# Token lists of the experts from 32-column one-hot matrices in four column groups, and a last expert in two halves

## The chip, the cores and the metric

The kernel runs on one core of one Trainium2 chip. The metric is device time in microseconds (us) of one execution, given as the median of several runs. The engines are named as in the profile: PE is TensorE's matmul, PEld its weight load, DVE VectorE, ACT ScalarE, POOL GpSimd, SP the engine whose queue carries most DMAs.

## What is computed

The reference is one adaptive-layer-norm block of a transformer: attention over 8 sequences of 1024 tokens with 256 features, then a mixture of 8 experts. The change lies in the mixture:

```python
logits = xf @ router_w + router_b                 # 8192 tokens x 8 experts
scores = softmax(logits)
G, idx = top_k(scores.T, 512)                     # each expert chooses 512 tokens
toks = xf[idx]
h1 = relu(einsum('ekh,ehf->ekf', toks, w1) + b1)  # 256 -> 1024
eo = einsum('ekf,efh->ekh', h1, w2) + b2          # 1024 -> 256
y = zeros.at[idx].add(eo * G)
```

An expert needs the list of its 512 tokens; the order within a list is free, since results are added back by token.

## The kernel before, in words

Up to about 3270 us the kernel does attention, the second layer norm and the router; up to 3333 us it searches, for all experts at once, the score that 512 tokens reach (fifteen rounds on DVE and PE), and numbers the tokens chosen. Each chosen token of an expert then has a slot from 0 to 511; a token that isn't chosen has slot -1. Tokens stand on 128 partitions, in 64 columns per expert: 4 blocks `i` (`KT`) by 16 columns `c` (`C`).

From there on the expert stage turns slots into a list. A slot is split into a low part `lo` (L954, 7 bits) and a high part `hi` (L955, 2 bits).

- `entries(e)` makes, on DVE, `at_hi` (L970, a one-hot of the high part over 4 values) and `ids` (L975 and L978): the number of the token, as the first token of its column (`first`) and its partition (`part`), put at the place of its high part. There are 8 columns for each of the 64.
- `choose(e, i)` makes `hot` (L985), a one-hot of the low part over 128 values for 16 columns, and multiplies: 16 matmuls (L992) with `hot` as the weights (128 columns) and `ids` as the moving operand (8 columns) add into `pi`, 128 slots x 8. It is called four times for an expert.
- `gather(e)` copies `pi` to `parts` (L1001), adds its halves to the token numbers `tok` (L1003), and issues four indirect DMAs on POOL (L1007), each fetching 128 rows with the normalized features, the router's scores and the gate.
- `turn(e)` transposes the rows on PE (L1020) and copies them to `xT` (L1023, DVE).
- `inner(e, f)`, 8 steps for an expert: two float32 matmuls (L1031) of 512 moving columns, each of them two passes in the profile, then bias and relu on ACT (L1035) into `h1`.
- `outer(e, j)`, for each of four groups of 128 tokens: 8 float32 matmuls (L1041) of 256 columns, then on DVE the bias (L1046) and the weighting by score and gate (L1047) into `eo`, and on POOL an indirect DMA (L1050) that adds `eo` to the output in DRAM. These scatters write the same tensor, and each waits for the landing of the one before.

The order of instructions in this stage is written by hand (`tc.manual_schedule()`): each engine issues in the order in which the code calls it. Ahead of the loop come `entries`, four `choose`, `gather` and `turn` of expert 0. In the period of expert `e`, the four `choose(e + 1, ...)` follow the inner steps 1, 3, 4 and 6 (counted from 0), `gather(e + 1)` follows the inner product, and `turn(e + 1)` follows the third outer step. Expert weights come in by DMA four experts ahead. In PSUM, `pi` has one bank, `px` two, `ph` three and `po` two. The setup of the constants (`iota_lo`, `iota_hi`, `part`, `first`, made on POOL) stands outside the written order, and a planner places it.

Of the kernel before, what the change touches and what calls it, by code (L numbers as in the profile page):

```python
# [28 lines left out]
F32 = mybir.dt.float32  # L29
BF16 = mybir.dt.bfloat16  # L30
I32 = mybir.dt.int32
AF = mybir.ActivationFunctionType
ALU = mybir.AluOpType
AX = mybir.AxisListType
# [3 lines left out]
P = 128  # L38
# [4 lines left out]
def adaln_block(  # L43
# [15 lines left out]
    nc = tc.nc  # L59
    B, S, D = x.shape  # L60
    H, _, _, N = w_qkv.shape
    E, _, F = w1.shape
    K = 512
# [5 lines left out]
    FC = F // P  # L69
    KT = K // P  # L70
# [7 lines left out]
    ident = const.tile([P, P], F32, name="ident")  # L78
# [14 lines left out]
    b1_sb = const.tile([P, E, FC], F32, name="b1_sb")  # L93
# [557 lines left out]
    def free_slot(g, behind=False):  # L651
        while g in taken or g % 4 == 0 or behind != (g % 4 == 3):
            g += 1
        taken.add(g)
        return g
# [9 lines left out]
    for b in range(B):  # L665
# [16 lines left out]
        if b + 1 < B:  # L682
# [3 lines left out]
            for t in range(NT):  # L686
                g = free_slot(64 * (b + 1) + 19 + 4 * t, True)
# [3 lines left out]
                if t % 2:  # L691
                    g = free_slot(g + 2, True)
                    at(g, "m2", out_turn, ps_m, b, t - 1)
                    g = free_slot(g + 1)
# [15 lines left out]
    with tc.manual_schedule():  # L710
# [20 lines left out]
        g = -1  # L731
# [96 lines left out]
    ex_w = {}  # L828

    def load_expert(e):  # L830
        w1_sb = wts.tile([P, KC, F], F32, tag="w1", name=f"w1_{e}")
        nc.sync.dma_start(w1_sb, w1[e].rearrange("(k p) f -> p k f", p=P))
        w2_sb = wts.tile([P, FC, D], F32, tag="w2", name=f"w2_{e}")
        nc.scalar.dma_start(w2_sb, w2[e].rearrange("(f p) d -> p f d", p=P))
        ex_w[e] = w1_sb, w2_sb
# [4 lines left out]
    rt = ctx.enter_context(tc.tile_pool(name="route", bufs=1))  # L840
    C = NTT // KT
    lo = rt.tile([P, KT, E, C], I32, name="lo")
    hi = rt.tile([P, KT, E, C], I32, name="hi")
    iota_lo = rt.tile([P, P], F32, name="iota_lo")
    iota_hi = rt.tile([P, KT], F32, name="iota_hi")
    part = rt.tile([P, 1], F32, name="part")
    first = rt.tile([P, KT, C], F32, name="first")
    b2_sb = rt.tile([P, E, D], F32, name="b2_sb")
# [5 lines left out]
    with tc.tile_pool(name="search", bufs=2) as se, tc.tile_pool(  # L854
        name="pos", bufs=1
    ) as po_, tc.tile_pool(name="se_ps", bufs=2, space=PSUM) as sps, tc.tile_pool(
        name="pos_ps", bufs=1, space=PSUM
    ) as pps:
        for dst, pattern, mult in (
            (iota_lo, [[1, P]], 0), (iota_hi, [[1, KT]], 0), (part, [[0, 1]], 1),  # L860
            (first, [[P, KT], [P * KT, C]], 0),
        ):
            i = po_.tile(list(dst.shape), I32, name=f"i_{dst.name}")
            nc.gpsimd.iota(i, pattern=pattern, base=0, channel_multiplier=mult)
            nc.gpsimd.tensor_copy(dst, i)

        whole = po_.tile([P, E, C], F32, name="whole")
        nc.gpsimd.memset(whole, 1.0)
# [24 lines left out]
        for s in range(15):  # L893
            bit = 28 - 2 * s
            cnt = se.tile([P, 3], F32, tag="cnt", name=f"cnt{s}")
            for k in range(3):
# [3 lines left out]
                    op0=ALU.is_ge, op1=ALU.add, accum_out=cnt[:, k : k + 1],  # L900
# [47 lines left out]
        for i in range(KT):  # L948
            nc.tensor.transpose(p_no[:, i, :], up[:, i * P : (i + 1) * P], ident)
        slot = po_.tile([P, KT, E, C], I32, name="slot")  # L950
        nc.vector.tensor_scalar_add(
            slot, p_no.rearrange("p i (e c) -> p i e c", e=E), -1.0
        )
        nc.vector.tensor_single_scalar(lo, slot, P - 1, op=ALU.bitwise_and)  # L954
        nc.vector.tensor_single_scalar(  # L955
            hi, slot, P.bit_length() - 1, op=ALU.arith_shift_right
        )

    ew = ctx.enter_context(tc.tile_pool(name="ework", bufs=2))
    ps_ids = ctx.enter_context(tc.tile_pool(name="ps_ids", bufs=1, space=PSUM))  # L960
    ps_x = ctx.enter_context(tc.tile_pool(name="ps_x", bufs=2, space=PSUM))
    ps_h = ctx.enter_context(tc.tile_pool(name="ps_h", bufs=3, space=PSUM))
    ps_o = ctx.enter_context(tc.tile_pool(name="ps_o", bufs=2, space=PSUM))
    out_rows = out.rearrange("b s d -> (b s) d")
    chosen = {}

    def entries(e):

        at_hi = ew.tile([P, KT, C, KT], F32, tag="at_hi", name=f"at_hi{e}")
        nc.vector.tensor_tensor(  # L970
            at_hi, hi[:, :, e, :].unsqueeze(3).to_broadcast([P, KT, C, KT]),
            iota_hi.unsqueeze(1).unsqueeze(1).to_broadcast([P, KT, C, KT]), ALU.is_equal,
        )
        ids = ew.tile([P, KT, C, 2 * KT], BF16, tag="ids", name=f"ids{e}")
        nc.vector.tensor_tensor(  # L975
            ids[:, :, :, :KT], at_hi, first.unsqueeze(3).to_broadcast([P, KT, C, KT]), ALU.mult
        )
        nc.vector.tensor_scalar(ids[:, :, :, KT:], at_hi, part, None, op0=ALU.mult)  # L978
        chosen[e] = ids, ps_ids.tile([P, 2 * KT], F32, tag="pi", name=f"pi{e}")

    def choose(e, i):

        ids, pi = chosen[e]
        hot = ew.tile([P, C, P], BF16, tag="hot", name=f"hot{e}_{i}")
        nc.vector.tensor_tensor(  # L985
            hot,
            iota_lo.unsqueeze(1).to_broadcast([P, C, P]),
            lo[:, i, e, :].unsqueeze(2).to_broadcast([P, C, P]),
            ALU.is_equal,
        )  # L990
        for c_ in range(C):
            nc.tensor.matmul(  # L992
                pi, hot[:, c_, :], ids[:, i, c_, :],
                start=(i == 0 and c_ == 0), stop=(i == KT - 1 and c_ == C - 1),
            )

    def gather(e):

        pi = chosen[e][1]
        parts = ew.tile([P, 2 * KT], F32, tag="parts", name=f"parts{e}")  # L1000
        nc.vector.tensor_copy(parts, pi)  # L1001
        tok = ew.tile([P, KT], I32, tag="tok", name=f"tok{e}")
        nc.vector.tensor_add(tok, parts[:, :KT], parts[:, KT:])  # L1003
        rows = []
        for j in range(KT):
            row = ew.tile([P, WIDE], F32, tag=f"row{j}", name=f"erow{e}_{j}")
            nc.gpsimd.indirect_dma_start(  # L1007
                out=row, out_offset=None, in_=rows_d,
                in_offset=bass.IndirectOffsetOnAxis(ap=tok[:, j : j + 1], axis=0),
            )  # L1010
            rows.append(row)
        chosen[e] = tok, rows

    def turn(e):
        tok, rows = chosen[e]
        xT = ew.tile([P, KC, K], F32, tag="xT", name=f"xT{e}")
        for k in range(KC):
            px = ps_x.tile([P, K], F32, tag="px", name=f"px{e}_{k}")
            for j in range(KT):
                nc.tensor.transpose(  # L1020
                    px[:, j * P : (j + 1) * P], rows[j][:, k * P : (k + 1) * P], ident
                )
            nc.vector.tensor_copy(xT[:, k, :], px)  # L1023
        h1 = ew.tile([P, FC, K], F32, tag="h1", name=f"h1_{e}")
        chosen[e] = tok, rows, xT, h1

    def inner(e, f):
        tok, rows, xT, h1 = chosen[e]
        ph = ps_h.tile([P, K], F32, tag="ph", name=f"ph{e}_{f}")
        for k in range(KC):  # L1030
            nc.tensor.matmul(  # L1031
                ph, ex_w[e][0][:, k, f * P : (f + 1) * P], xT[:, k, :],
                start=(k == 0), stop=(k == KC - 1),
            )
        nc.scalar.activation(h1[:, f, :], ph, AF.Relu, bias=b1_sb[:, e, f : f + 1])  # L1035

    def outer(e, j):
        tok, rows, xT, h1 = chosen[e]
        po = ps_o.tile([P, D], F32, tag="po", name=f"peo{e}_{j}")
        for f in range(FC):  # L1040
            nc.tensor.matmul(  # L1041
                po, h1[:, f, j * P : (j + 1) * P], ex_w[e][1][:, f, :],
                start=(f == 0), stop=(f == FC - 1),
            )
        eo = ew.tile([P, D], F32, tag="eo", name=f"eo{e}_{j}", bufs=4)
        nc.vector.tensor_add(eo, po, b2_sb[:, e, :])  # L1046
        nc.vector.scalar_tensor_tensor(  # L1047
            eo, eo, rows[j][:, D + e : D + e + 1], rows[j][:, ROW:], op0=ALU.mult, op1=ALU.mult
        )
        nc.gpsimd.indirect_dma_start(  # L1050
            out=out_rows,
            out_offset=bass.IndirectOffsetOnAxis(ap=tok[:, j : j + 1], axis=0),
            in_=eo, in_offset=None, compute_op=ALU.add,
        )


    with tc.manual_schedule():
        entries(0)
        for i in range(KT):
            choose(0, i)  # L1060
        gather(0)
        turn(0)
        for e in range(E):
            more = e + 1 < E
            if more:
                entries(e + 1)
            for f in range(FC):
                inner(e, f)
                if more and f in (1, 3, 4, 6):
                    choose(e + 1, (1, 3, 4, 6).index(f))  # L1070
            if more:
                gather(e + 1)
            for j in range(KT):
                outer(e, j)
                if more and j == 2:
                    turn(e + 1)
            if e + 4 < E:
                load_expert(e + 4)


# [29 lines left out]
```

## Time and profile before

| | us |
|---|---|
| median of 3 runs | 3617.36 (3617.17 to 3618.96) |
| profiled execution | 3616.66 |
| its span, first to last instruction | 3614.9 |
| PE busy | 3458.4 (96%) |
| DVE busy | 2898.9 (80%) |
| POOL busy | 2660.0 (74%) |
| ACT busy | 2439.8 (67%) |
| first instruction of the expert stage starts | 3333.62 |
| inner product of the first and of the last expert starts | 3354.68, 3575.0 |
| last scatter is issued | 3607.31 |

All positions are microseconds from the start of the span. In a line of instructions, the name `hot<-iota_lo,lo` says which tile is written from which; the shapes are partitions x elements per partition; "x16" is how many instructions the line holds. Brackets give the idle time of the engine ahead of the line, and what ended it. A busy matmul includes the pipeline's latency, so the pace of PE is read from starts, not from durations. The granted TensorE clock is 1.0 at full rate; in the search and at the start of the expert stage it is 0.5.

### The profile page before, as it was taken

The numbers are of one execution on the slowest core, as the hardware profiler recorded it, in microseconds if no ns is written. First come the engines' busy times: TensorE is split into PE (matmuls) and PEld (weight loads), VectorE is DVE, ScalarE is ACT, GpSimd is POOL, SyncE is SP. The second block draws the span as 40 slices with busy tenths as digits, with TensorE's granted clock in tenths as the row PEclk, the third lists the DMA queues.
The fourth block names the chain that finished last, engine by engine and source line by source line (L and its number), as shares of the span: only waits on it lengthen the run. The fifth ranks groups of instructions, "written<-read, shape, count | busy, mean of one in ns | idle before, by whom it ended". The sixth has DMA issues, their size and how long they took to land. (4 is left out here: it accounts for less than half of the span.)

```text
span 3614.9 us, 54207 instructions
## 1 busy us (share of the span) xinstructions
PE 3458.4 (96%) x20622; PEld 1456.3 (40%) x20622; DVE 2898.9 (80%) x3641; ACT 2439.8 (67%) x2988; POOL 2660.0 (74%) x1537
## 2 busy tenths in 40 slices
PE   7999999999999999999999999999999999982898
PEld 3333333343433443344433434334334344342565
DVE  5888888888888888888888888888888888857442
ACT  4777777777777777777777777777777777730111
POOL 2778777887788887977888788877888877851332
PEclk9999999999999999999999999999999999995999
DMA  3010012011111113111211112011201112133332
GB/s 77 13 42 31 25 32 67 29 45 45 59 50 35 51 49 64 31 39 51 61 46 44 41 44 62 30 52 48 67 29 45 45 59 49 51 87 121 94 100 41
DMA packets 189652, 185.39 MB, mean 51 GB/s; under 512 B 48952, under 2 KB 167240, under 8 KB 189264
## 3 DMA queue, kind: packets, MB, share of 16 engines
q1 hardware_dynamic: 173616, 160.29, 15.5%
q0 software_dynamic: 7168, 12.72, 1.7%
q10 hardware_dynamic: 8608, 8.92, 0.8%
q8 instruction: 162, 2.65, 0.3%
q14 instruction: 98, 0.80, 0.1%
HBM read 127.06 MB, written 63.21 MB: 53 GB/s over the span
## 5 line engine op out<-in xcount | busy, mean ns | idle before, releaser
L457 POOL TENSOR_TENSOR acc<-acc,p 128x1024 f32<-128x1024 f32 x762 | 1806.6, 2371 | 361.2 <-ACT p L429 328.1
L376 ACT COPY p<-s 128x1024 f32<-128x1024 f32 x1024 | 997.2, 1020 | 417.8 <-PE s L367 407.7
L426 DVE TENSOR_TENSOR p<-p,less 128x1024 f32<-128x1024 f32 x1024 | 1206.8, 1210 | 32.5 <-PE less L423 30.0
L381 DVE TENSOR_TENSOR top<-top,s 128x1024 f32<-128x1024 f32 x768 | 936.9, 1220 | 276.5 <-ACT p L376 236.2
L429 ACT ACTIVATE p<-p 128x1024 f32<-128x1024 f32 x1024 | 1042.8, 1058 | 73.7 <-DVE p L426 73.4
L367 PE MATMUL s<-qk,qk 64*128 64x512 f32 x4096 | 1025.1, 612 | 34.0 <-DVE parts L404 31.0
L438 PE MATMUL av<-p,v 128*64 128x512 f32 x4096 | 967.1, 593 | 1.8 <-ACT oT L447 1.8
L367 PEld LDWEIGHTS s<-qk,qk 64*128 64x128 f32 x4096 | 358.7, 186 | 527.8 <-issue 241.2
L332 PE MATMUL pq<-hT,wq 128*64 128x512 f32 x2048 | 498.4, 608 | 2.7 <-ACT v L354 2.1
L438 PEld LDWEIGHTS av<-p,v 128*64 128x64 f32 x4096 | 280.5, 137 | 461.4 <-issue 366.2
L454 POOL TENSOR_TENSOR acc<-p,p 128x1024 f32<-128x1024 f32 x127 | 301.8, 2376 | 178.0 <-ACT p L429 178.0
L332 PEld LDWEIGHTS pq<-hT,wq 128*64 128x64 f32 x2048 | 124.8, 136 | 342.4 <-issue 210.8
L349 PE MATMUL pv<-wq,hT 128*64 128x256 f32 x2048 | 249.3, 385 | 0.7 <-ACT qk L337 0.7
L1035 ACT ACTIVATE h<-ph,b_sb 128x512 f32<-128x512 f32 x64 | 44.1, 689 | 274.7 <-PE ph L1031 274.7
L396 DVE TENSOR_REDUCE tt<-tt 128x8 f32<-128x1024 f32 x128 | 157.4, 1230 | 69.6 <-PE tt L388 69.5
L548 PE MATMUL po<-wo,ot 128*64 128x256 f32 x1792 | 205.7, 382 | 0.0
L349 PEld LDWEIGHTS pv<-wq,hT 128*64 128x64 f32 x2048 | 135.6, 136 | 153.3 <-issue 65.9
L381 DVE TENSOR_TENSOR top<-p,s 128x1024 f32<-128x1024 f32 x128 | 155.8, 1217 | 14.5 <-ACT p L376 14.5
L388 PEld LDWEIGHTS tt<-ident,top 128*128 128x128 f32 x1024 | 109.6, 140 | 106.6 <-DVE top L381 105.8
L519 POOL TENSOR_TENSOR oT<-oT,rb 128x1024 f32<-128x1024 f32 x63 | 150.1, 2382 | 3.0 <-DMA rb<-rden_d 3.0
L548 PEld LDWEIGHTS po<-wo,ot 128*64 128x64 f32 x1792 | 123.6, 137 | 66.1 <-issue 9.4
L388 PE MATMUL tt<-ident,top 128*128 128x128 f32 x1024 | 139.9, 280 | 2.6 <-DVE top L381 2.6
(166 smaller groups left out, 2357.3 us busy)
## 6 DMA issues: line engine op xcount, KB each, us to landing
rb<-rden_d SPq DMA_DIRECT2D x128, 256.0 KB
oT_d<-oT SPq DMA_DIRECT2D x62, 512.0 KB
ot<-oT_d SPq DMA_DIRECT2D x56, 512.0 KB
rows_d<-row SPq DMA_DIRECT2D x64, 132.0 KB
rows_d<-gb_d SPq DMA_DIRECT2D x8, 1024.0 KB
w<-in_L_ffn_w_dram ACTq DMA_DIRECT2D x8, 1024.0 KB
w<-in_L_ffn_w_dram SPq DMA_DIRECT2D x8, 1024.0 KB
lnx<-in_L_attn_inputs_dram SPq DMA_DIRECT2D x28, 256.0 KB
```

Of the source, the lines that this page charges most:

```text
L332: nc.tensor.matmul(pq[m * N : (m + 1) * N, :], wq_of(k, a, 2 * p + m), hTs[b][:, k, sl], start=(k == 0), stop=(k == KC - 1),)
L349: nc.tensor.matmul(pv[m * N : (m + 1) * N, i, :], hTs[b][:, k, t0 : t0 + N], wq_of(k, 2, 4 * g, 4), start=(k == 0), stop=(k == KC - 1),)
L367: nc.tensor.matmul(ps[:, j, :], kt[r, c * P : (c + 1) * P], qt[r, h * QB : (h + 1) * QB], start=True, stop=True,)
L376: nc.scalar.copy(probs[u, c], ps)
L381: nc.vector.tensor_tensor(tops[u], probs[u, 0] if c == 1 else tops[u], ps, ALU.max)
L388: nc.tensor.transpose(turned[u][:, 4 * j + t, :], top[:, j, t * P : (t + 1) * P], ident)
L426: nc.vector.tensor_tensor(probs[u, c], probs[u, c], less[u], ALU.add)
L429: nc.scalar.activation(probs[u, c], probs[u, c], AF.Exp)
L438: nc.tensor.matmul(avs[u][j * N : (j + 1) * N, :], v[:, c, hh * N : (hh + 1) * N], pT[:, j, :], start=(c == 0), stop=(c == NT - 1),)
L454: nc.gpsimd.tensor_tensor(sums[u], pts[0], pts[1], ALU.add)
L457: nc.gpsimd.tensor_tensor(sums[u], sums[u], pt, ALU.add)
L548: nc.tensor.matmul(po[m * N : (m + 1) * N, :], ot[:, p, m * N : (m + 1) * N], wo[:, p, :], start=(p == 0), stop=(p == NP - 1),)
```

## The change

The slot is split at 5 bits rather than 7. `hot` becomes one tile for the whole expert, a one-hot of the low part over 32 values, and `at_hi` and `ids` grow to 16 values of the high part: `ids` has 32 columns for each of the 64. `choose(e)` is called once. Its 64 matmuls have 32 weight columns each and are dealt out to four column groups of PE (`tile_position`), each of which adds up a quarter of the columns in 32 partitions of `pi`. The result is copied as bfloat16 to `parts` (exact, since its numbers are small or multiples of 128 with few bits). `gather(e)` first folds: 8 matmuls with the 0/1 matrix `fold` (32 columns, made once from the identity) add the four groups and both halves of the number, and put 4 high values into each group of 32 partitions, so that `tok` again is 128 x 4. `tok` is then one copy from PSUM.

In the loop, `choose(e + 1)` follows inner step 4 and `gather(e + 1)` inner step 5. The last expert leaves the loop: it does all inner steps for its first 256 tokens, then their two outer steps, then the same for the other 256.

```diff
@@ setup
-    iota_lo = rt.tile([P, P], F32, name="iota_lo")
-    iota_hi = rt.tile([P, KT], F32, name="iota_hi")
+    LO = 32
+    HI = K // LO
+    iota_lo = rt.tile([P, LO], F32, name="iota_lo")
+    iota_hi = rt.tile([P, HI], F32, name="iota_hi")
+    fold = rt.tile([P, LO], BF16, name="fold")
...
-            (iota_lo, [[1, P]], 0), (iota_hi, [[1, KT]], 0), (part, [[0, 1]], 1),
+            (iota_lo, [[1, LO]], 0), (iota_hi, [[1, HI]], 0), (part, [[0, 1]], 1),
...
+        nc.vector.tensor_reduce(
+            fold, ident.rearrange("p (g l) -> p l g", l=LO), AX.X, ALU.max
+        )
...
-        nc.vector.tensor_single_scalar(lo, slot, P - 1, op=ALU.bitwise_and)
+        nc.vector.tensor_single_scalar(lo, slot, LO - 1, op=ALU.bitwise_and)
         nc.vector.tensor_single_scalar(
-            hi, slot, P.bit_length() - 1, op=ALU.arith_shift_right
+            hi, slot, LO.bit_length() - 1, op=ALU.arith_shift_right
         )
@@ def entries(e)
-        at_hi = ew.tile([P, KT, C, KT], F32, tag="at_hi", name=f"at_hi{e}")
+        hot = ew.tile([P, KT, C, LO], BF16, tag="hot", name=f"hot{e}")
         nc.vector.tensor_tensor(
-            at_hi, hi[:, :, e, :].unsqueeze(3).to_broadcast([P, KT, C, KT]),
-            iota_hi.unsqueeze(1).unsqueeze(1).to_broadcast([P, KT, C, KT]), ALU.is_equal,
-        )
-        ids = ew.tile([P, KT, C, 2 * KT], BF16, tag="ids", name=f"ids{e}")
+            hot, iota_lo.unsqueeze(1).unsqueeze(1).to_broadcast([P, KT, C, LO]),
+            lo[:, :, e, :].unsqueeze(3).to_broadcast([P, KT, C, LO]), ALU.is_equal,
+        )
+        at_hi = ew.tile([P, KT, C, HI], BF16, tag="at_hi", name=f"at_hi{e}")
         nc.vector.tensor_tensor(
-            ids[:, :, :, :KT], at_hi, first.unsqueeze(3).to_broadcast([P, KT, C, KT]), ALU.mult
-        )
-        nc.vector.tensor_scalar(ids[:, :, :, KT:], at_hi, part, None, op0=ALU.mult)
-        chosen[e] = ids, ps_ids.tile([P, 2 * KT], F32, tag="pi", name=f"pi{e}")
-
-    def choose(e, i):
-        ids, pi = chosen[e]
-        hot = ew.tile([P, C, P], BF16, tag="hot", name=f"hot{e}_{i}")
+            at_hi, hi[:, :, e, :].unsqueeze(3).to_broadcast([P, KT, C, HI]),
+            iota_hi.unsqueeze(1).unsqueeze(1).to_broadcast([P, KT, C, HI]), ALU.is_equal,
+        )
+        ids = ew.tile([P, KT, C, 2 * HI], BF16, tag="ids", name=f"ids{e}")
         nc.vector.tensor_tensor(
-            hot,
-            iota_lo.unsqueeze(1).to_broadcast([P, C, P]),
-            lo[:, i, e, :].unsqueeze(2).to_broadcast([P, C, P]),
-            ALU.is_equal,
-        )
-        for c_ in range(C):
-            nc.tensor.matmul(
-                pi, hot[:, c_, :], ids[:, i, c_, :],
-                start=(i == 0 and c_ == 0), stop=(i == KT - 1 and c_ == C - 1),
-            )
+            ids[:, :, :, :HI], at_hi, first.unsqueeze(3).to_broadcast([P, KT, C, HI]), ALU.mult
+        )
+        nc.vector.tensor_scalar(ids[:, :, :, HI:], at_hi, part, None, op0=ALU.mult)
+        chosen[e] = hot, ids
+
+    def choose(e):
+        hot, ids = chosen[e]
+        pi = ps_ids.tile([P, 2 * HI + KT], F32, tag="pi", name=f"pi{e}")
+        for i in range(KT):
+            for c_ in range(C):
+                r = c_ % 4 * LO
+                nc.tensor.matmul(
+                    pi[r : r + LO, : 2 * HI], hot[:, i, c_, :], ids[:, i, c_, :],
+                    start=(i == 0 and c_ < 4), stop=(i == KT - 1 and c_ >= C - 4),
+                    tile_position=(0, r),
+                )
+        parts = ew.tile([P, 2 * HI], BF16, tag="parts", name=f"parts{e}")
+        nc.vector.tensor_copy(parts, pi[:, : 2 * HI])
+        chosen[e] = parts, pi
 
     def gather(e):
-        pi = chosen[e][1]
-        parts = ew.tile([P, 2 * KT], F32, tag="parts", name=f"parts{e}")
-        nc.vector.tensor_copy(parts, pi)
+        parts, pi = chosen[e]
+        for g in range(4):
+            r = g * LO
+            for i in range(2):
+                nc.tensor.matmul(
+                    pi[r : r + LO, 2 * HI :], fold, parts[:, i * HI + g * KT : i * HI + (g + 1) * KT],
+                    start=(i == 0), stop=(i == 1), tile_position=(0, r),
+                )
         tok = ew.tile([P, KT], I32, tag="tok", name=f"tok{e}")
-        nc.vector.tensor_add(tok, parts[:, :KT], parts[:, KT:])
+        nc.vector.tensor_copy(tok, pi[:, 2 * HI :])
@@ def inner
-    def inner(e, f):
+    def inner(e, f, t0=0, n=K):
...
-                ph, ex_w[e][0][:, k, f * P : (f + 1) * P], xT[:, k, :],
+                ph, ex_w[e][0][:, k, f * P : (f + 1) * P], xT[:, k, t0 : t0 + n],
...
-        nc.scalar.activation(h1[:, f, :], ph, AF.Relu, bias=b1_sb[:, e, f : f + 1])
+        nc.scalar.activation(
+            h1[:, f, t0 : t0 + n], ph, AF.Relu, bias=b1_sb[:, e, f : f + 1]
+        )
@@ the written order
         entries(0)
-        for i in range(KT):
-            choose(0, i)
+        choose(0)
         gather(0)
         turn(0)
-        for e in range(E):
-            more = e + 1 < E
-            if more:
-                entries(e + 1)
+        for e in range(E - 1):
+            entries(e + 1)
             for f in range(FC):
                 inner(e, f)
-                if more and f in (1, 3, 4, 6):
-                    choose(e + 1, (1, 3, 4, 6).index(f))
-            if more:
-                gather(e + 1)
+                if f == FC // 2:
+                    choose(e + 1)
+                if f == FC // 2 + 1:
+                    gather(e + 1)
             for j in range(KT):
                 outer(e, j)
-                if more and j == 2:
+                if j == 2:
                     turn(e + 1)
             if e + 4 < E:
                 load_expert(e + 4)
+        for i in range(2):
+            for f in range(FC):
+                inner(E - 1, f, i * K // 2, K // 2)
+            for j in range(KT // 2):
+                outer(E - 1, i * KT // 2 + j)
```

More of the change, by code (lines that the diff above doesn't have):

```diff
@@ L1025, in turn @@
         chosen[e] = tok, rows, xT, h1
-    def inner(e, f):
+    def inner(e, f, t0=0, n=K):
         tok, rows, xT, h1 = chosen[e]
-        ph = ps_h.tile([P, K], F32, tag="ph", name=f"ph{e}_{f}")
+        ph = ps_h.tile([P, n], F32, tag="ph", name=f"ph{e}_{f}_{t0}")
         for k in range(KC):
             nc.tensor.matmul(
-                ph, ex_w[e][0][:, k, f * P : (f + 1) * P], xT[:, k, :],
+                ph, ex_w[e][0][:, k, f * P : (f + 1) * P], xT[:, k, t0 : t0 + n],
                 start=(k == 0), stop=(k == KC - 1),
             )
-        nc.scalar.activation(h1[:, f, :], ph, AF.Relu, bias=b1_sb[:, e, f : f + 1])
+        nc.scalar.activation(
+            h1[:, f, t0 : t0 + n], ph, AF.Relu, bias=b1_sb[:, e, f : f + 1]
+        )
     def outer(e, j):
```

## The prediction

> **What bounds the kernel now.** I first read the page's busy shares (TensorE 96%, VectorE 80%) and the slices. Nothing before the expert stage (from 3333 us) changes but two constants, so I then cut that stage into pieces and asked of each which engine its end waits for. The windows view of one expert's period (columns: window, length, then busy us of PE, PEld, DVE, ACT, POOL, then granted clock, DMA share, GB/s):
>
> ```profile
> 3386.00:3417.40 31.40, 30.54 (x170) 20.56 (x169) 15.09 (x19) 5.51 (x8) 11.88 (x8) 1.00 0.43 118
> ```
>
> TensorE is busy for 30.5 of 31.4 us, so whatever it is spared here comes off the time, and what other engines are spared does not. What it does with the one-hot product is in the timeline of the second expert (start us, length, engine, group, in brackets the idle time before it and who ended it):
>
> ```profile
> 3388.63 6.69 DVE L985 TENSOR_TENSOR hot<-iota_lo,lo 128x2048 bf16<-128x2048 f32 x3
> ...
> 3390.15 0.69 ACT L1035 ACTIVATE h<-ph,b_sb 128x512 f32<-128x512 f32 x1 [1.03 <-PE ph L1031]
> ...
> 3390.97 0.56 PE L992 MATMUL pi<-ids,hot 128*128 128x8 bf16 x16 [0.86 <-DVE hot L985]
> ...
> 3393.39 0.69 ACT L1035 ACTIVATE h<-ph,b_sb 128x512 f32<-128x512 f32 x1 [2.55 <-PE ph L1031]
> 3395.11 0.69 ACT L1035 ACTIVATE h<-ph,b_sb 128x512 f32<-128x512 f32 x1 [1.03 <-PE ph L1031]
> ...
> 3397.31 0.69 ACT L1035 ACTIVATE h<-ph,b_sb 128x512 f32<-128x512 f32 x1 [1.52 <-PE ph L1031]
> ```
>
> The ACT starts are a clock for the inner product: 1.72 us a step without a choose (3393.39 to 3395.11), 2.20 with one (to 3397.31), so a choose costs TensorE 0.48 to 0.49 us. The first choose of an expert costs 3.24 - 1.72 = 1.52: 1.03 more, because its matmuls wait for the first `hot`. Experts 2 to 7 (six periods of 31.41, from ACT and PE starts 31.4 apart) show the same 3.24; in the first period that step is 2.21, without a wait. The sum closes: inner product 8 x 1.716 = 13.73, outer product 4 x 3.45 = 13.80, turn 0.88, together 28.4; with 4 x 0.49 + 1.03 it is 31.4.
>
> At both ends TensorE doesn't set the time. The first expert's list is a serial chain at half clock:
>
> ```profile
> 3333.62 0.42 DVE L970 TENSOR_TENSOR at_hi<-hi,iota_hi 128x256 f32<-128x256 int32 x1
> 3334.08 0.42 DVE L975 TENSOR_TENSOR ids<-at_hi,first 128x256 bf16<-128x256 f32 x1
> 3334.42 0.35 DVE L978 TENSOR_SCALAR ids<-at_hi,part 128x256 bf16<-128x256 f32 x1
> 3334.68 8.89 DVE L985 TENSOR_TENSOR hot<-iota_lo,lo 128x2048 bf16<-128x2048 f32 x4
> ...
> 3343.63 0.59 PE L992 MATMUL pi<-ids,hot 128*128 128x8 bf16 x16 [1.61 <-DVE hot L985]
> ...
> 3344.45 0.16 DVE L1003 TENSOR_TENSOR tok<-parts 128x4 int32<-128x4 f32 x1
> 3345.61 1.25 POOL L1007 DMA_INDIRECT erow<-rows_d,tok  x1 [73.76 <-DVE tok L1003]
> ```
>
> And the end is a chain of four scatters, 4.5 to 4.6 us apart, longer than an outer step of 3.45 us, so the last starts 4.6 us after its rows' VectorE work began:
>
> ```profile
> 3593.61 1.55 POOL L1050 DMA_INDIRECT out_dram<-eo,tok  x1 [13.26 <-DVE eo L1047]
> 3598.10 1.55 POOL L1050 DMA_INDIRECT out_dram<-eo,tok  x1 [2.94 <-issue]
> 3602.72 1.55 POOL L1050 DMA_INDIRECT out_dram<-eo,tok  x1 [3.07 <-issue]
> 3602.74 0.42 DVE L1046 TENSOR_TENSOR eo<-peo,b_sb 128x256 f32<-128x256 f32 x1 [2.51 <-PE peo L1041]
> 3607.31 1.55 POOL L1050 DMA_INDIRECT out_dram<-eo,tok  x1 [3.03 <-issue]
> ```
>
> **What the Trainium skill says.** "TensorEngine Tiling (Array Packing)", Key Properties: tiles run independently, and changing the tiling mode drains TensorE. The trace agrees on both, with the softmax sums (4 column groups, float32, 256 columns):
>
> ```profile
> 3204.72 0.16 PEld L473 LDWEIGHTS pd_last<-p,ones 128*32 128x32 f32 x8 [0.81 <-issue]
> 3204.73 0.64 PE L473 MATMUL pd_last<-p,ones 128*32 128x256 f32 x8
> 3205.29 0.20 PEld L438 LDWEIGHTS av<-p,v 128*64 128x64 f32 x4 [0.41 <-ACT p L429]
> ```
>
> Eight passes hold TensorE for 0.57 us, where the outer product pays 0.2155 for each pass of that size (1.72 for eight): the groups overlap. Record by record, passes of different groups start 7 ns apart, and two rounds of 0.213 leave about 0.15 of the 0.57; about 0.09 more passes before the block. So two switches cost about 0.24, and 0.3 with a float32 weight load of 128 columns then uncovered. "TensorE: Matmul & The Clock Gate", Weight-path perf modes: the fast weight load needs 128 columns and no float32, so 32 columns lose it. No run here shows the new shape; the nearest is the router (L600, 64 float32 columns, two groups, 8 moving columns): its records show 58 ns a round, 29 a pair, at full clock. "VectorE: DVE Perf Modes", Mode 2x_2P: a tensor_scalar can do two elements a cycle, a tensor_tensor in float32 one. Here L954 does 512 int32 elements in 0.34, `hot` 2048 in 2.22 from start to start: it agrees.
>
> **The change, part by part.**
>
> *TensorE per period.* Removed: 4 x 0.49 = 1.96, and the wait of 1.03 if nothing replaces it. Added: 64 pairs in 16 rounds of four groups, 32 columns each. Lower bound 0.88: eight instructions a round at 7 ns, 55 ns. Upper bounds: pairs that don't overlap, 25 ns as now (1.6), or 29 as in the router (1.86). I take 0.88, since the pd records overlap by group in the very same tile shape, and a load and multiply of 32 columns should be shorter than the router's 58 ns round, whose loads are twice as wide. With 0.3 for the switches, 1.18. The fold is 8 pairs, two after each other in each group: 0.25 and again 0.3 of switches, 0.55 (to 0.8). Sum 1.73. Gain: 3.01 - 1.73 = 1.28 in six periods, 1.96 - 1.73 = 0.23 in the first (no wait there): 7.9 us. With the upper bounds (2.16 + 0.8 = 2.96) it is 6 x 0.05 - 1.0 = -0.7.
>
> *Does a new wait replace the old?* VectorE per period: `hot` 2.22; `at_hi` now 1024 elements, 1.07 + 0.19 for the dependence; product 1.14; last one 0.75 at two a cycle (1.15 at one). Together 5.4 (5.8), against 10 before. It starts after the previous expert's last `eo` at 3387.65, ends at 3393.1 to 3393.5; the choose after the fifth inner step comes at 3386.51 + 5 x 1.716 = 3395.1. Cover 1.6 us; beyond it each us is paid six times. Behind a choose on TensorE stand the remaining inner steps, and behind those ACT and everything else. The fold's wait for `parts` (about 0.2 + 0.2) lies under an inner step of 1.72; were that cover gone, 0.4 a period. The copy to `tok` is as long as the add it replaces. The gathers start about 3 us earlier (near 3399.8 against 3402.8): worth nothing, since the turn at the third outer step already finds the rows there in every period but the first. On POOL the gathers stand before the same scatters as now; the fourth scatter of the expert before, which now waits beside `hot` until 3393.4 and then takes 3.32, must be over by then, and has fewer large VectorE operations to meet. POOL is busy for 12 of 31 us.
>
> *First expert.* `hot` can start at 3333.5; 5.37 later, 3338.87, TensorE starts. At half clock a round, a load of 32 and a minimum pair, may take 77 ns (my estimate from the router's half-clock rounds of 104): 1.23 + 0.17 to drain, 3340.3; `parts` 0.2, fold 0.5, `tok` 0.2, with handovers: 3341.4 against 3344.6. Gain 3.2; 1.5 if pairs take 54 ns, 2.8 if the last VectorE operation runs at one a cycle. The clock came back at full rate 2.7 us after the inner product's start (3354.68 to about 3357.4); where that falls after a shift can move the end by up to 1.5 us either way.
>
> *Last expert.* Inner halves of 256 columns load weights twice as often, but the outer product runs exactly such passes at 0.2155 with loads under them: 2 x 6.9 us, the same 13.8; ACT has 16 operations of about 0.42 (0.69 less 256 elements) under steps of 0.86. Outer rows 3 and 4 still end when they do: 27.96 after the start at 3574.78. But scatter 3 no longer stands behind 1 and 2, long over: it starts at 24.51 + 1.22 = 25.73, the fourth 4.6 later at 30.3, against 32.53. Gain 2.2. If ACT or a second load costs TensorE 0.1 a step, 0.6.
>
> *Setup.* One reduction of 128 elements, about 0.3, and smaller iotas; VectorE idles 2.6 us before 3269.88 while the routing runs. Nothing; 0.3 if placed on the routing chain.
>
> Sum: 7.9 + 3.2 + 2.2 = 13.3 us. The profiled execution took 3616.66 (span 3614.9 and 1.8 around it), so 3603.4; the median is 0.7 higher: **3604.0**.
>
> **Rivals.** (1) The column groups don't overlap at this size, since each pair needs its own issue, and nothing is loaded fast: choose 1.9 to 2.2. Against it stand the 7 ns starts. Gain 5 to 9 us, 3608 to 3612. (2) A new wait for VectorE: `at_hi` and `ids` at half rate through strided bfloat16 writes, 3.4 us more, less 1.6 of cover, times six: 11 of the gain goes, and 3.4 at the first expert: 3618. The present `ids`, strided as well, run at one a cycle, which speaks against it; half of that effect gives 3611. (3) Slower: the 64 narrow loads and multiplies stall each other within a group. Break-even: 5.4 us from the two ends and 6 x 3.01 + 1.96 = 20.0 now spent leave 3.6 us a period; less 0.3 + 0.55, 43 ns a pair. At 60 ns it would be 3626. The router's 29 ns speaks against it. (4) The clock's return slips by one step: 3605.5, inside the likeliest case.
>
> **How the numbers follow.** About 0.2% of the time, 7.2 us, is what a measurement of this kernel tells from no change, so faster means under 3610.1 and slower above 3624.6. Likeliest case 0.68 (own range 3601 to 3607); rival 1 0.16, three quarters of it under 3610; rival 2 0.08, seldom under it; rival 3 0.08. Faster 0.68 + 0.12 + 0.01, 0.81; slower 0.07, same 0.12. The range to 3610.5 takes in most of rival 1; below, 3600.5 allows 17 us, if rounds and switches are cheaper still.
>
> **What would show it.** The 128x32 passes of one choose starting 14 ns or less apart on average; a period near 29.9 (between ph starts); no wait of a choose for VectorE; `tok` of the first expert near 3341; last scatter 30.3 after the last expert's start. I am wrong if the choose takes over 2 us, if TensorE waits for `ids` or `parts`, or if the halved inner product takes more than 14 us.

## The result

| | before | after |
|---|---|---|
| median, 6 runs each (us) | 3617.69 (3615.82 to 3618.96) | 3598.56 (3597.54 to 3600.32) |
| profiled execution | 3616.66 | 3597.83 |
| its span | 3614.9 | 3596.1 |

The ratio is 0.9948, with a 95% interval of 0.9938 to 0.9959: 19.1 us less, where 13.3 were forecast. The direction was right. The median lies 1.9 us below the stated range of 3600.5 to 3610.5, so the range missed.

Laid side by side at five marks of the two traces, the spans differ as follows.

| stretch | before | after | gain | forecast |
|---|---|---|---|---|
| start of the span to `hi` (nothing of the list's making has run) | 3333.09 | 3332.44 | 0.65 | 0 |
| `hi` to the first expert's `tok` | 11.36 | 6.97 | 4.39 | 3.2 |
| `tok` to the first inner product | 10.23 | 10.21 | 0.02 | 0 |
| first period (first inner product to the second) | 31.83 | 31.38 | 0.45 | 0.23 |
| six periods | 6 x 31.41 | 6 x 29.56 | 11.1 | 7.7 |
| last inner product's start to the last scatter | 32.31 | 30.10 | 2.21 | 2.2 |
| last scatter to the end of the span | 7.59 | 7.63 | -0.04 | 0 |

The gains sum to 18.8 us, the difference of the spans. The first line is no effect of the list code. Attention is the same in both programs, and the first copies of its scores already start 0.46 us earlier, by the middle of the run 0.54. In the fourteen profiles of this document `hi` starts anywhere from 3332.1 to 3335.1 us, whatever the kernel. Without these 0.65 us the median would still lie below the range.

**The profile after.** The windows view of one period (the columns are those of the prediction's first fence):

```profile
3381.00:3410.56 29.56, 29.56 (x178) 19.61 (x177) 10.15 (x16) 5.50 (x8) 9.83 (x9) 1.00 0.47 126
```

TensorE has no idle time left in the period, and VectorE works 10.15 us instead of 15.09. The timeline shows where the product now stands:

```profile
3386.66 0.48 DVE L990 TENSOR_SCALAR ids<-at_hi,part 128x1024 bf16<-128x1024 bf16 x1
...
3388.07 0.69 ACT L1053 ACTIVATE h<-ph,b_sb 128x512 f32<-128x512 f32 x1 [1.03 <-PE ph L1049]
...
3389.67 0.66 PE L1001 MATMUL pi<-ids,hot 128*32 128x32 bf16 x64
3389.78 0.69 ACT L1053 ACTIVATE h<-ph,b_sb 128x512 f32<-128x512 f32 x1 [1.03 <-PE ph L1049]
...
3390.43 0.19 DVE L1007 CAST parts<-pi 128x32 bf16<-128x32 f32 x1 [3.29 <-PE pi L1001]
...
3392.18 0.22 PE L1016 MATMUL pi<-parts,fold 128*32 128x4 bf16 x8
3392.29 0.69 ACT L1053 ACTIVATE h<-ph,b_sb 128x512 f32<-128x512 f32 x1 [1.82 <-PE ph L1049]
...
3394.35 0.69 ACT L1053 ACTIVATE h<-ph,b_sb 128x512 f32<-128x512 f32 x1 [1.38 <-PE ph L1049]
```

Read the ACT starts as a clock again. A step without extra work is 1.72 us. The step with the choose is 2.51, so the choose costs 0.79. The step with the fold is 2.06, so the fold costs 0.345. Together they cost 1.14 us, where the four old chooses and the wait cost 3.01. VectorE is done at 3387.14, 2.5 us before the choose begins, and no wait stands before it.

The first list, again at half clock:

```profile
3332.97 2.29 DVE L977 TENSOR_TENSOR hot<-iota_lo,lo 128x2048 bf16<-128x2048 f32 x1
3335.18 1.22 DVE L982 TENSOR_TENSOR at_hi<-hi,iota_hi 128x1024 bf16<-128x1024 int32 x1
...
3336.43 1.22 DVE L987 TENSOR_TENSOR ids<-at_hi,first 128x1024 bf16<-128x1024 bf16 x1
3337.57 0.48 DVE L990 TENSOR_SCALAR ids<-at_hi,part 128x1024 bf16<-128x1024 bf16 x1
3338.11 0.69 PE L1001 MATMUL pi<-ids,hot 128*32 128x32 bf16 x64 [6.77 <-DVE ids L990]
...
3339.41 0.16 DVE L1021 CAST tok<-pi 128x4 int32<-128x4 f32 x1 [0.34 <-PE pi L1016]
3340.48 1.25 POOL L1025 DMA_INDIRECT erow<-rows_d,tok  x1 [69.22 <-DVE tok L1021]
```

And the end, where two scatters now stand where four stood:

```profile
3583.96 1.55 POOL L1070 DMA_INDIRECT out_dram<-eo,tok  x1 [7.82 <-DVE eo L1067]
...
3588.47 1.55 POOL L1070 DMA_INDIRECT out_dram<-eo,tok  x1 [2.95 <-issue]
```

### The profile page after: what moved, and what is told of

It reads as the page before. It is cut to its first block, busy times and chain, and to the rows that moved or that the text cites. A ratio compares the mean times of both kernels' runs of the same rounds, so it can differ in the third digit from the quotient of the medians.

```text
span 3596.1 us, 54368 instructions
## 1 busy us (share of the span) xinstructions
PE 3450.2 (96%) x20718; PEld 1454.7 (40%) x20718; DVE 2859.3 (80%) x3618; ACT 2438.7 (68%) x2996; POOL 2652.1 (74%) x1537
## 5 line engine op out<-in xcount | busy, mean ns | idle before, releaser
L1053 ACT ACTIVATE h<-ph,b_sb 128x512 f32<-128x512 f32 (+1 forms) x72 | 46.0, 639 | 263.5 <-PE ph L1049 263.5
```

## The experiments

The theory after the result had four parts, and each was put to the test:

- the wait for `hot` had cost what the trace of before showed, and is gone;
- the product is cheaper than priced, because column groups overlap;
- the pieces of the change add up;
- the halves of the last expert give their 2.2 us by themselves.

The rivals were that one of the two loop effects made the whole gain, and that narrow weights are cheap without any groups. Runs 1 to 4 shared one chip, 5 to 8 another and 9 to 11 a third, and run 12 stood alone, each batch beside its own runs of the kernel before (medians 3617.70, 3616.91, 3617.09 and 3617.05); ratios are to these. The changed kernel's 3598.56 comes from the runs of the result, so differences of about 1 us between its median and that of another run tell nothing. A period is the time between the starts of two inner products in the one profiled execution of each run. In most runs the six periods agree to 0.02 us (exceptions are named), and so tell finer differences than medians, whose runs lie 1 to 7 us apart.

### 1. The halves alone

Kernel before, with the changed `inner` and this end of the loop:

```diff
-        for e in range(E):
+        for e in range(E - 1):
...
+        for i in range(2):
+            for f in range(FC):
+                inner(E - 1, f, i * K // 2, K // 2)
+            for j in range(KT // 2):
+                outer(E - 1, i * KT // 2 + j)
```

> The kernel before with one part of the change alone: the last expert in two halves. Theory: the fourth scatter no longer stands behind the first and the second, 2.2 us faster than before, 3615.5 us; the halved inner product of the last expert takes TensorE 13.8 us as the whole one did. Rival: the tail is hidden or the halved weights cost what the tail gives, 0.0 to 0.6 us, 3617 to 3617.7.

Measured: 3615.20 us, ratio 0.9992 (0.9984 to 1.0). In the trace the last expert takes 30.19 us from its start to its last scatter, against 32.31. That is 2.1 us, as in the changed kernel. The median alone would not settle so small a step, but the trace does.

### 2. The wait alone

```diff
-                if more and f in (1, 3, 4, 6):
-                    choose(e + 1, (1, 3, 4, 6).index(f))
+                if more and f in (2, 3, 4, 5):
+                    choose(e + 1, (2, 3, 4, 5).index(f))
```

> The kernel before, its four choose calls after the inner steps 2, 3, 4 and 5 instead of 1, 3, 4 and 6, nothing else. The hot tiles are then ready when TensorE gets there. Theory: the wait of 1.03 us goes from six periods, the product stays: 6.2 us faster than before, 3611.5 us, a period of 30.4. Rival (the loop's gain comes from the cheaper product alone, and the wait is paid elsewhere): no change, 3617.7.

Measured: 3611.14 us, ratio 0.9983 (0.9976 to 0.999), 6.6 us less. The period is 30.37, against 31.41. TensorE's idle time is gone from the window:

```profile
3387.91:3418.29 30.38, 30.38 (x170) 20.65 (x169) 14.99 (x19) 5.50 (x8) 11.56 (x9) 1.00 0.45 122
```

So 1.04 of the 1.85 us that a period gained are the wait. They could be had by moving four calls, with the product as it was. The other 0.81 are the product.

### 3. The lists alone

Changed kernel with the last expert inside the loop again, whole:

```diff
-        for e in range(E - 1):
-            entries(e + 1)
+        for e in range(E):
+            more = e + 1 < E
+            if more:
+                entries(e + 1)
```

> The changed kernel with the last expert whole, as before. Theory: the parts are additive, so it loses the 2.2 us of the tail: 3600.8 us, 16.9 us faster than before. Rival: the halves only pay, or pay more, with the new lists: not within 1 us of that.

Measured: 3600.51 us, ratio 0.9952 (0.9939 to 0.9966), 17.2 us less than before. With the 2.5 of run 1 this makes 19.7, against 19.1 for both together. The parts add up within the spread.

### 4. Column groups in turn

```diff
-                r = c_ % 4 * LO
+                r = c_ // 4 * LO
...
-                    start=(i == 0 and c_ < 4), stop=(i == KT - 1 and c_ >= C - 4),
+                    start=(i == 0 and c_ % 4 == 0), stop=(i == KT - 1 and c_ % 4 == 3),
```

> The changed kernel, the same 64 matmuls of a choose, but four in a row go to one column group before the next group has its four. Theory (the gain rests on neighbouring pairs lying in different groups, a group being free again only after 25 to 33 ns): 1.6 to 2.1 us for a choose instead of 0.55, over eight lists 8 to 12 us slower than the changed kernel, 3607 to 3611 us. Rival (narrow weights are simply issued faster, 8 to 9 ns a pair wherever they go): no change from it, 3598.6 us.

Measured: 3598.52 us, ratio 0.9948 (0.9935 to 0.9962), a period of 29.66. The theory had said 8 to 12 us slower; it is 0.10 us a period. So the theory, as worded, fell. Either TensorE overlaps groups over runs of at least four pairs, or the groups don't matter. Runs 9 and 10 tell these apart.

### 5. The product twice

```diff
+        for again in range(2):
             for i in range(KT):
                 for c_ in range(C):
```

> The changed kernel with the 64 matmuls of each choose done twice (the second pass starts the sums anew, so the list is the same). This prices the product by itself. Theory: 8.3 to 9.2 ns a pair as the trace of the changed kernel shows, 0.53 to 0.59 us a list, eight lists: 4.2 to 4.7 us slower than the changed kernel, 3603 us. Rival (the pair costs 14 ns as predicted, and the rest of the loop's gain comes from elsewhere): 7 us slower, 3605.7.

Measured: 3603.31 us, ratio 0.9961 (0.9947 to 0.9974), against 3598.56 for the changed kernel. Five of the six periods are 30.10 (one is 30.18): 0.54 us more than 29.56 for 64 pairs more, 8.4 ns a pair. The predicted 14 ns is out.

### 6. The wait put back

```diff
-                if f == FC // 2:
+                if f == 2:
                     choose(e + 1)
```

> The changed kernel with the choose after inner step 2 instead of 4, where VectorE isn't done with the one-hot matrices: this puts a wait back. Theory: VectorE ends 6.1 us after the start of a period, step 2 ends after 5.15, so TensorE waits 1.0 us in six periods (none in the first, which starts at half clock): 6 us slower than the changed kernel, 3604.6. Rival (a wait of TensorE is caught up later in the period): no change, 3598.6.

Measured: 3604.92 us, ratio 0.9967 (0.9955 to 0.9979), 6.4 us slower than the changed kernel. The period is 30.52 in five of six. The fourth took 31.85. The waiting product in the timeline, in the second period and then in the fourth:

```profile
3387.04 0.48 DVE L990 TENSOR_SCALAR ids<-at_hi,part 128x1024 bf16<-128x1024 bf16 x1
...
3387.57 0.66 PE L1001 MATMUL pi<-ids,hot 128*32 128x32 bf16 x64 [0.88 <-DVE ids L990]
...
3448.61 0.59 PE L1001 MATMUL pi<-ids,hot 128*32 128x32 bf16 x56 [0.89 <-DVE ids L990]
3449.65 0.23 PE L1001 MATMUL pi<-ids,hot 128*32 128x32 bf16 x6 [0.45 <-issue]
```

In the fourth period the product stopped behind its 56th pair and again six pairs later, and took 1.33 us longer from first to last start than in the others. That is the whole difference; why it stopped is not shown. The five others have an idle time of 0.88 before the product, and 0.96 more in the period than the changed kernel. A wait of TensorE in this loop is paid in full. With run 2 that holds in both directions, once with the old product and once with the new.

### 7. The fold at once

```diff
-                if f == FC // 2 + 1:
+                if f == FC // 2:
                     gather(e + 1)
```

> The changed kernel with the fold and the gathers directly behind the choose, no inner step between. This saves one entry into and one exit from the 32-column mode, and lays the copy to parts open. Theory: the copy is ready 0.45 us after TensorE has issued the last pair, more than the 0.2 us of the switches: 0.25 us a period slower, 1.5 to 2 us in all, 3600.3. Rival (the switches are the dearer part, as the predicted 0.3 us a block said): 0 to 1 us faster, 3598.

Measured: 3599.84 us, ratio 0.9953 (0.9939 to 0.9966). The period is 29.77, 0.21 longer than 29.56 in every one of six.

```profile
3392.61 0.66 PE L1001 MATMUL pi<-ids,hot 128*32 128x32 bf16 x64
...
3393.36 0.19 DVE L1007 CAST parts<-pi 128x32 bf16<-128x32 f32 x1 [3.29 <-PE pi L1001]
3393.61 0.22 PE L1016 MATMUL pi<-parts,fold 128*32 128x4 bf16 x8 [0.33 <-DVE parts L1007]
```

The copy, which the changed kernel hides under an inner step, now stands open. It costs more than the spared entry and exit of the 32-column mode.

### 8. The first expert in halves too

`turn` is split into two halves of 256 tokens, and the first expert's inner product with it:

```diff
-        turn(0)
+        turn_half(0, 0)
...
+            if e == 0:
+                for f in range(FC):
+                    inner(e, f, 0, K // 2)
+                turn_half(0, 1)
             for f in range(FC):
-                inner(e, f)
+                if e == 0:
+                    inner(e, f, K // 2, K // 2)
+                else:
+                    inner(e, f)
```

> The changed kernel with the first expert's inner product in two halves of its tokens too: the first half starts when two of its four groups of rows have landed. Theory: TensorE starts 2.6 us earlier; part of that is lost to half clock and to the second turn standing in the product: 1 to 2.6 us faster than the changed kernel, 3596 to 3597.6. Rival (the clock's return decides, one step of 3.4 us later or earlier): between 0.7 us slower and 3 us faster.

Measured: 3596.83 us (3596.21 to 3597.38), ratio 0.9944 (0.993 to 0.9957), 1.7 us below the changed kernel. From `tok` to the inner product is 7.24 us, against 10.21. The first period grows from 31.38 to 32.14 in return, because half of the turn now stands in it: 0.99 us, with a wait of 0.39 for its copy. The clock took some of that back, since it returned 2.7 us after the start and not 3.5. Counted from `hi` to the end of the span, the two traces differ by 2.2 us.

### 9 and 10. One group, two groups

```diff
-                r = c_ % 4 * LO
+                r = 0          # two groups: r = c_ % 2 * LO
...
-        nc.vector.tensor_copy(parts, pi[:, : 2 * HI])
+        nc.vector.tensor_copy(parts[:LO], pi[:LO, : 2 * HI])   # two: 2 * LO
```

> The changed kernel with all 64 matmuls of a choose in one column group (the other three groups of parts are set to zero beforehand). With the groups in turn the choose cost only 0.10 us more, so either the groups overlap over stretches longer than four pairs, or narrow weights alone make the pair cheap. Theory (groups overlap; one group takes a new pair after 25 to 33 ns): 1.6 to 2.1 us a choose, 8 to 12 us over eight lists, 3607 to 3611 us, periods of 30.6 to 31.1. Rival (32 weight columns alone): 8 to 10 ns a pair, periods of 29.6 to 29.7, 3598.6 to 3599.5.

> The changed kernel with the 64 matmuls of a choose dealt out to two column groups instead of four. Theory: 32 rounds of 25 to 33 ns, 0.8 to 1.05 us a choose, 0.25 to 0.5 us more, 2 to 4 us over eight lists, 3600.6 to 3602.6, periods of 29.8 to 30.1. Rival (32 weight columns alone): as with four groups, 29.56 to 29.7.

Measured: one group 3607.53 us, ratio 0.9975 (0.9965 to 0.9984), with a period of 30.67; two groups 3600.24 us, ratio 0.9956 (0.9942 to 0.9969), with a period of 29.87. The products in the timelines of one group and of two:

```profile
3390.96 1.77 PE L1003 MATMUL pi<-ids,hot 128*32 128x32 bf16 x64
```

```profile
3390.28 0.97 PE L1003 MATMUL pi<-ids,hot 128*32 128x32 bf16 x64
```

From first to last start, record by record, a pair takes 25.2 ns in one group, 12.6 in two and 7.6 in four. Times 64 this is 1.13 and 0.32 us more than with four groups, and the periods are 1.11 and 0.31 longer. The old pair of 128 weight columns and 8 moving ones took 25.3 ns. So a quarter of the weight columns, with four times the moving ones, was worth nothing by itself: one column group takes a new pair every 25.2 ns, and two groups take exactly twice as many. With four the pace is 7.6 instead of 6.3, or 9.3 when they come in turn (run 4). The overlap of groups carries the gain of the product, but it doesn't need neighbouring pairs in different groups.

### 11. One block, and what it cost

Both halved experts, and the lists begun two periods ahead, so that the fold of one stands directly ahead of the choose of the next. Both lists' sums lie in one PSUM tile:

```diff
-                if f == FC // 2:
-                    choose(e + 1)
-                if f == FC // 2 + 1:
+                if f == (FC - 2 if e == 0 else FC // 2):
                     gather(e + 1)
+                    if e + 2 < E:
+                        choose(e + 2)
...
```

> Both halved experts as in the run before of that name, and the list of an expert begun two periods ahead, so that its fold stands directly ahead of the choose of the next list: one entry into the 32-column mode and one exit less in five periods. Theory: 0.2 us in each, a period of 29.37, 1 us less than with both halves alone, 3595.8 us. Rival (the fold's 0.35 us is its matmuls, not the switch): 29.5 us or more, 3596.8.

Measured: 3631.98 us, ratio 1.0045 (1.0031 to 1.0059), 35 us slower than run 8 and slower than the kernel before. Its timeline:

```profile
3394.87 0.16 DVE L1023 CAST tok<-pi_all 128x4 int32<-128x4 f32 x1 [4.16 <-DMA out_dram<-eo,tok]
3395.08 0.51 PE L1003 MATMUL pi_all<-ids,hot 128*32 128x32 bf16 x46 [1.61 <-DVE tok L1023]
...
3395.87 0.23 PE L1003 MATMUL pi_all<-ids,hot 128*32 128x32 bf16 x6 [0.28 <-issue]
3396.61 0.22 PE L1003 MATMUL pi_all<-ids,hot 128*32 128x32 bf16 x5 [0.51 <-issue]
```

The windows view of the same kernel, from just before that choose to the end of the slow clock:

```profile
3393.20:3398.10 4.90, 1.52 (x73) 0.96 (x72) 0.16 (x1) 0.69 (x1) 2.19 (x3) 0.99 0.36 75
3398.10:3401.50 3.40, 3.40 (x5) 1.51 (x5) 0.19 (x1) 0.00 (x0) 1.70 (x2) 0.51 0.72 186
```

Neither expectation had this. The token numbers have two buffers, and the older one is still being read by a scatter in flight. The copy to `tok` waits for that scatter, and the choose waits for the copy, since both use the one tile `pi_all`: 1.78 us from the fold's last start to the choose's first. Behind the wait only the first 46 of the 64 pairs keep their pace, and the rest come in bursts, 2.5 us in all more than the 0.5 of an unbroken product. After that the clock is at half for one window of 3.4 us, 1.7 us of work. The three make 6.0; the period shown is 35.15, 5.9 more than the 29.28 of run 12.

The scatter is the smaller part of this. At the first and at the last of the six lists that come behind a fold, no scatter stands in the way. The first of them:

```profile
3364.14 0.51 PE L1003 MATMUL pi_all<-ids,hot 128*32 128x32 bf16 x46 [0.28 <-DVE tok L1023]
```

Here the choose starts 0.45 us after the fold's last start and waits for the copy alone. The pace breaks all the same (3.0 us from first to last start), half clock follows, and each of these two periods is 4.7 us longer than in run 12. In the four periods between, the scatter adds 1.1 to 2.3 us of waiting, and in two of these half clock lasted 6.8 us (periods of 36.8). Why the pace breaks stays open. A wait alone doesn't do it: the first list of the changed kernel stood behind 6.77 us of idle time and kept its pace, and so did five of the six waiting products of run 6. Nor does the number of pairs: run 5's 128 came without such stops.

### 12. The fold behind the choose

Against run 11:

```diff
                 if f == (FC - 2 if e == 0 else FC // 2):
-                    gather(e + 1)
                     if e + 2 < E:
                         choose(e + 2)
+                    add(e + 1)        # the fold
+                    gather(e + 1)     # tok, three buffers, and the gathers
+                    if e + 2 < E:
+                        take(e + 2)   # the copy to parts
...
```

> As the run with one block, but the choose of the next list comes first and the fold of the present list directly behind it, and the token numbers have three buffers. So TensorE waits neither for the copy of the token numbers nor for a scatter that still reads the older ones. Theory (the 36 us that the one block lost all hang on that wait: the wait itself, the broken pace of the pairs behind it, and a window at half clock): the wait is gone, a period is 29.37, 0.2 us less than in the changed kernel in five periods, 3595.8 us. Rival (the pace breaks because two lists are in flight, whatever the order): periods of 32 and more, over 3612 us.

Measured: 3595.36 us (3594.09 to 3598.89), ratio 0.9941 (0.9928 to 0.9955), the fastest of all, 22 us under the kernel before and 3.2 under the changed one, of which the halves of the first expert give about half (1.7 in run 8).

```profile
3389.34 0.66 PE L1001 MATMUL pi_all<-ids,hot 128*32 128x32 bf16 x64
...
3389.83 0.25 PE L1018 MATMUL pi_all<-parts,fold 128*32 128x4 bf16 x8
3390.16 0.16 DVE L1026 CAST tok<-pi_all 128x4 int32<-128x4 f32 x1 [3.36 <-PE pi_all L1018]
```

The period is 29.28, 0.28 less than in the changed kernel (the last of the six, which has no choose, takes 28.77, and so prices the 64 pairs alone at 0.51): an entry and an exit of the 32-column mode cost 0.28 us, so of the fold's 0.345 only 0.07 is its eight matmuls. With the wait gone, the broken pace and the slow clock of run 11 are gone too. That the pace broke because two lists are in flight is thereby out. The order and the third buffer were changed together; what each does alone was not tried.

## Why the prediction was right and wrong

**The wait (1.03 us in six periods): right.** It was read from the ACT starts, and run 2 took it away alone for 1.04 a period. Its price at full value was right as well: run 6 put 0.96 of it back. Rival 2, a new wait for VectorE, did not come: VectorE's chain took 5.08 us, where 5.4 to 5.8 were forecast, and ended 2.5 us before the choose, where the forecast had 1.6.

**The price of the product: wrong, and this is the step that failed.** The prediction took a choose at 0.88 + 0.3 us and the fold at 0.25 + 0.3, 1.73 together. Measured are 0.79 and 0.345, 1.14. The 0.3 for the switches was right (0.28 by run 12). The terms mis-sized are the pairs: 0.88 became 0.51, and 0.25 became 0.07. This is 0.56 to 0.59 us in each of six periods, the 3.4 us missing there. The mechanism, overlap of column groups, was right by runs 9 and 10; only its size was off, and part of it could have been read correctly. In the softmax sums of the kernel before, the records of one pass and of the next group's pass start 7 ns apart, with the load of each inside these 7 ns. The prediction took 7 ns as the price of one instruction, counted eight instructions for a round of four pairs, and called the 55 ns a lower bound. The same records say 28 ns a round for the issue; the run showed 30. They don't say how soon a group can take its next pair: that came from run 9, 25.2 ns, and so just fits into the round. A bound that was none also cut the range off at the bottom.

**The first list: right in kind, 1.2 us short.** VectorE's chain took 5.08 us instead of 5.37, since the last operation (L990) took 0.48 and not 0.75, with bfloat16 in and out. From TensorE's first pair to the copy of `parts` took 0.76 instead of 1.4: the estimate that a round takes longer at half clock failed, since a pair takes 7.9 ns there and 7.6 at full clock. The router's rounds, from which it was drawn, do lengthen, from 58 ns to 107 (the prediction has 104), but they are of another shape and type. The rest, to the end of `tok`, took 0.7 instead of 1.1. About half of what was missing, then, is again the price of the pairs.

**The first period: 0.45 instead of 0.23.** 1.96 less 1.14 would be 0.82. The clock came back 3.48 us after the inner product's start and not 2.75, which at half rate costs 0.37. The forecast had named this as a shift of up to 1.5 us without taking a side.

**The tail: right**, 2.21 against 2.2, and the same 2.1 alone in run 1. **The gathers' earlier start: worth nothing, as said**, since no period but the first waits for rows. **The setup: right.** The reduction takes 0.37 us while VectorE waits for the routing.

**The other rivals.** That groups don't overlap was out by runs 9 and 10. A stall within a group (43 ns and more a pair over all) was far off: a pair took 7.6 ns, and with all of them in one group 25.2. The 0.65 us with which the span began earlier belongs to the spread between runs.

## What to carry to other kernels

Before costing narrow matmuls, read from records of the same tile shape how far apart whole pairs of load and multiply start: that interval holds both instructions. Where one engine is full, look first for its idle gaps: 1.04 of the 1.85 us that a period gained could be had by calling the first product one inner step later, and the last one step earlier. When work is moved ahead on the engine that sets the time, look at what it now stands behind, and follow the buffers to their last reader: a product behind the copy of the token numbers cost 4.7 us a period, with a scatter still reading an older list 5.6 to 7.5, and another order with a third small buffer took all of it away.

## What the runs showed that was not expected

- A column group takes a pair every 25.2 ns, as long as the whole array took for the old pair with 128 weight columns (25.3). Two groups give 12.6 and four 7.6 ns, nearly as well (9.3) when four pairs in a row go to one group.
- For such short pairs the granted clock hardly matters: 7.9 ns at half clock, 7.6 at full.
- Entry to and exit from the 32-column mode cost 0.28 us together, four times what eight short matmuls in it cost.
- In run 11 each of the six waits of TensorE, 0.45 to 2.7 us long, with a broken product of 3.0 us behind it, was followed by 3.4 or 6.8 us at half clock. In run 6 a wait of 0.9 us with a broken product of 1.8 us was not.
